# A transformer block on one core: the MLP's row preparation from batch 6 on, rearranged between ScalarE, VectorE and GpSimd

## The chip, the core and the metric

The kernel runs on one core of a Trainium2 chip. A core has five engines that run at the same time, each through its own list of instructions in order: TensorE (PE in the profile; PEld is its loading of weights), VectorE (DVE), ScalarE (ACT), GpSimd (POOL) and SyncE (SP), which here issues the DMA transfers. They wait for each other through semaphores. SBUF is the on-chip memory of 128 partitions, PSUM the small memory into which TensorE writes its products.

The metric is the device time of one execution in microseconds, the median of several runs. Beside it stands one execution taken by the hardware profiler, from which every row below comes.

## The reference, cut to what matters

`x` is 16 batches of 256 tokens by 256 channels, `cond_1024` one vector of 256 per batch, `ctx_1024` 16 x 256 x 256. All is float32. The block is

```python
shift_a, scale_a, gate_a, shift_m, scale_m, gate_m = split(silu(c) @ W_mod + b_mod, 6)
x = x + gate_a * (self_attention(modulate(ln(x), shift_a, scale_a)) @ W_proj + b_proj)
x = x + cross_attention(ln(x), ln(context)) @ W_cproj + b_cproj
x_norm2 = ln(x) * (1 + scale_m) + shift_m          # one scale and one shift per batch and channel
h = gelu(x_norm2 @ W_mlp1 + b_mlp1)                # 256 -> 1024 channels
x = x + gate_m * (h @ W_mlp2 + b_mlp2)             # 1024 -> 256 channels
```

Both attentions have 16 heads. The change touches only the last three lines, for the batches 6 to 15.

## The kernel before, in words

**Precision.** TensorE multiplies in a reduced float32 format (fp32r). To come close to float32, each operand is split into a high part (the value cast to fp32r) and a low part (value minus high part, again cast), and a product is made of three: high x high, high x low, low x high. So every tile that goes into a product needs a cast and a subtraction first.

**Stages.** First the 32 attention units (self and cross for 16 batches) run in an order written out by hand; each cross unit writes its batch's rows to a DRAM buffer `x2d`. Then comes a bridge (the word list `BE`), in which the last attention unit and the MLP of the batches 0 to 2 are interleaved. Then a loop over chunks does the MLP from batch 3 on. A batch has four chunks of 256 hidden channels (`NCH` = 4); iteration (b,c) is chunk c of batch b. Each engine gets its instructions in exactly the order in which the program issues them, so the loop's order is the order on every queue.

**A chunk.** Iteration (b,c) issues, for the chunk list counted by i:

- `mlp_gelu(i+1)`: ScalarE reads the first product `ph` from PSUM twice, each time as two halves of 128x256, into `hf` (float32) and `hh` (fp32r, the high part); GpSimd makes `hl = hf - hh`, 128x512;
- `mlp_first(i+2)`: TensorE, 12 matmuls into `ph`, from the rows' parts (`wcross`, see below) and the first weights (`wself`). There are two PSUM buffers for `ph`, so the first product of chunk i+2 needs `mlp_gelu(i)` to be finished;
- `mlp_second(i-1)`: TensorE, 12 matmuls into `st` or `sp` (`s` in the rows; the batches alternate), from `hh`, `hl` and the second weights (`big`). After a batch's last chunk VectorE multiplies by the gate (`mt`, two instructions), adds (`y`), and SP stores the result.

**The rows of a batch.** What `mlp_first` needs is the batch's normalised, scaled and shifted rows, turned so that channels lie on partitions, as high and low part. They stand in two alternating places, `ROWS[b % 2]`, both parts of the tile `wcross`. They come about as follows:

1. `mlp_load` (SP): the batch's rows from `x2d` into `xt`, `x` in the rows;
2. `mlp_bias`: adds `cb`, a bias row that is the same for all tokens, to `xt` in place (one 128x512 instruction, GpSimd);
3. `mlp_stats`: VectorE's mean and variance (`st_m`, `mv_m`);
4. `ln.pow`: GpSimd makes 1/sqrt(variance + eps) (`rs_m`, two small instructions); `mlp_nb`: VectorE makes the negated mean times that (`nb_m`);
5. `ln.steps[2]("act")`: ScalarE normalises, two Identity activations 128x256 into `xn_m`;
6. the turn. For the batches up to 5 (`TURN` is 6) `mlp_T` turns by TensorE, scales by VectorE and casts the high part by ScalarE. From batch 6 on `mlp_turn` has VectorE transpose 32x32 blocks (two instructions, into `z`), and SP moves the blocks between partitions with four DMAs of 64 KB (`yT<-z`);
7. `mlp_turned`, from batch 6 on: VectorE scales and shifts `yT` back into `z` (two instructions 128x256), casts the high part (128x512) and subtracts for the low part (128x512).

Besides, `mlp_gates` (SP) loads the batch's gate rows `gm`, and `mlp_residual` has VectorE prepare `xmg = x + ` a gate row (128x512).

**The order around the change.** For d = 6 and later the steps before stood so: bias at (d-3,0) (for d = 6 at (3,1)), statistics one iteration later, power at (d-3,3), negated mean and normalise at (d-2,0), turn at (d-2,1), at the end of that iteration and behind the store, the gates and the next load on SP, `mlp_turned` at (d-1,0). The first product that reads the rows is issued at (d-1,2). In the profile every instruction has line 51, that of a helper that issues all of them; rows are told apart by tile names.

The functions that the diff touches, and what calls them:

Of the kernel before, what the change touches and what calls it, by code (L numbers as in the profile page):

```python
# [21 lines left out]
def pixart_block(  # L22
# [8 lines left out]
    B, N, H = x.shape  # L31
# [4 lines left out]
    KC = H // P  # L36
# [15 lines left out]
                return tc.keep_in_program_order(i) if self.on else i  # L52
            return issue

    E_ = {'CUT': 8, 'LN': {'s': 'pool', 'c': 'pool', 'q': 'pool'}, 'ON': (1, 1, 1), 'L0': -16, 'L1': 1, 'S0': -7, 'A0': 0, 'T0': 1, 'S1': 5, 'A1': 7, 'L2': 9, 'T1': 9, 'S2': 32, 'AP': 99, 'DV': (0, 1), 'HP': (1, 0), 'BZ': {}, 'AV': {1: [(1, 2), (1, 3)], 9: [(0, 0), (0, 1)]}, 'AHEAD': (0, 0, 0, 0, 0, 2), 'TW': {(21, 6): 'cb', (23, 5): 'u0', (23, 7): 'u1', (25, 2): 'u2', (27, 3): 'u3', (27, 7): 'h2a', (28, 0): 'l2 h0p u5', (28, 2): 'h1p', (28, 4): 'h3p', (28, 7): 'u4 u6', (29, 0): 'l3d', (29, 1): 'l0', (29, 2): 'l1', (29, 7): 'h5p', (30, 1): 'u7 h6d h7p', (30, 3): 'h4p', (31, 1): 'l4 l6d', (31, 2): 'l5d x2', (31, 4): 'l7', (31, 7): 'b2'}, 'BE': 'G0 av P g0 A1 G1 G2 N1 F7 g1 S0 PF s2 p2 G3 a2 aT aL G4 x3 b3 S1 S2 T2 C r0 G5 S3 G6 S4 s3 CF x4 F8 g2 G7 S5 F9 p3 S6 G8 a3 r1 G9 F10 G10 T3 g3 b4 S7 s4 F11 S8 S9 F12 G11 p4 a4 F13 r2 S10 G12 x5 x6', 'XP': 1, 'IL': 1, 'MF': 0, 'SH': 4, 'RAMP': 1, 'HA': 1, 'MP': 16, 'W': (7, 1, 0, 0), 'PRE': 'load L0a z0kp z0qp L0b silu b15 hik turn L0d brow bp lok T0t lg scale b6 lc sc1 ld2 L1a T0h one0 z1kp bro2 T0l hiv hiq shift b3 K0a L1b bk K0m bq loq K0h b1 L1d K0l Q0a L2a T1t T1h lp K0yp K0x Q0m T1l bv K1a lov Q0h K0w V0a Q0l K1b Q1a L2b Q0x Q1b Q0w Q1l K1y V0b Q0yp b7 K1l ld3', 'SL': {(-1, 0): 'wm one1 L2c z1qp', (-1, 1): 'T2t T2h V1a', (-1, 2): 'K1wp T2p', (-1, 3): 'ga K1xp L3a Q1yp V1b z2kp', (-1, 4): 'M0 Q1xp Q1wp pb L3b vone gs', (-1, 5): 'z2qp ld4', (-1, 6): 'K2a K2m L3p', (-1, 7): 'L3c cb lx gm', (0, 0): 'sp3 mods', (0, 1): 'sp0', (0, 3): 'sp1', (0, 4): 'sc2', (0, 6): 'one2', (1, 1): 'sp2', (1, 2): 'sp4'}}

    PE = InOrder(nc.tensor, True)
    ACT, DVE, POOL, SP = (InOrder(e, True) for e in (nc.scalar, nc.vector, nc.gpsimd, nc.sync))
# [51 lines left out]
    brow = const.tile([32, P], F32, name="brow")  # L110
# [11 lines left out]
    def split(hi, lo, src, eng=POOL, hp=0):  # L122
        (DVE, POOL, ACT)[E_['HP'][hp]].tensor_copy(hi, src) if E_['HP'][hp] < 2 else ACT.copy(hi, src)
        eng.tensor_tensor(lo, src, hi, ALU.subtract)
# [173 lines left out]
    wm = []  # L298
# [9 lines left out]
    gm = []  # L308
# [19 lines left out]
    def layernorm(src, name):  # L328
# [282 lines left out]
    def bc_t(ap):  # L611
        return ap.unsqueeze(1).to_broadcast([P, NT, H])
# [226 lines left out]
    M = {}  # L839
# [6 lines left out]
        SP.dma_start(m.xt, tok(X2d, b))  # L846
        m.ln = layernorm(lambda: m.xt, f"m{b}")

    def mlp_bias(b):
        POOL.tensor_tensor(M[b].xt, M[b].xt, bc_t(cb), ALU.add)  # L850

    def mlp_stats(b, power=False):
        M[b].ln.steps[0]()
        M[b].ln.steps[1](power)

    def mlp_nb(b):
        ln = M[b].ln
# [14 lines left out]
    def mlp_residual(b):  # L872
        m = M[b]
        m.xg = work.tile([P, NT, H], F32, tag="x1", name=f"xmg_{b}", bufs=7)
        DVE.tensor_tensor(m.xg, m.xt, bc_t(m.g[:, 1]), ALU.add)

    def mlp_T(b):

        m = M[b]
        pst = ps_gen(f"psT_m{b}", SHORT)  # L880
        for f in range(KC):
            for t in range(NT):
                PE.transpose(pst[:, f * N + t * P:f * N + (t + 1) * P],
                             m.ln.xn[:, t, f * P:(f + 1) * P], ident)
        y = work.tile([P, KC, N], F32, tag="y", name=f"xTf_m{b}", bufs=2)
        hi, lo = ROWS[b % 2]
        for f in range(KC):
            DVE.tensor_scalar(y[:, f], pst[:, f * N:(f + 1) * N], sc1[:, 1, f, b:b + 1],
                              cpT[:, 6 + f, b:b + 1], ALU.mult, ALU.add)
        if b in E_['DV']:  # L890
            DVE.tensor_copy(hi, y)
        else:
            for f in range(KC):
                ACT.activation(hi[:, f], pst[:, f * N:(f + 1) * N], AF.Identity,
                               bias=cpT[:, 6 + f, b:b + 1], scale=sc1[:, 1, f, b:b + 1])
        DVE.tensor_tensor(lo, y, hi, ALU.subtract)
        m.xT = (hi, lo)

    TURN = 6

    def mlp_turn(b):


        m = M[b]
        m.z = work.tile([P, 4, KC, NT * 32], F32, tag="xn", name=f"z_{b}", bufs=3)
        m.y = work.tile([P, 4, KC, NT * 32], F32, tag="y", name=f"yT_{b}", bufs=2)
        for t in range(NT):
            DVE.transpose(m.z[:, :, :, 32 * t:32 * t + 32].rearrange("p j k c -> p k j c"),
                          m.ln.xn[:, t].rearrange("p (k c j) -> p k j c", k=KC, j=4))
        for a in range(4):  # L910
            SP.dma_start(m.y[:, a].rearrange("p k c -> p (k c)"),
                         m.z[32 * a:32 * a + 32].rearrange("r j k c -> r j (k c)"))

    def mlp_turned(b):

        m = M[b]
        hi, lo = m.xT = ROWS[b % 2]
        for f in range(KC):
            DVE.tensor_scalar(m.z[:, :, f], m.y[:, :, f], sc1[:, 1, f, b:b + 1],
                              cpT[:, 6 + f, b:b + 1], ALU.mult, ALU.add)  # L920
        y = m.z.rearrange("p a k c -> p k a c")
        hi, lo = [w.rearrange("p k (a c) -> p k a c", a=4) for w in (hi, lo)]
        DVE.tensor_copy(hi, y)
        DVE.tensor_tensor(lo, y, hi, ALU.subtract)

    NCH = NF // 2

# [112 lines left out]
    u0, u1 = units[:2]  # L1040
# [4 lines left out]
    u2 = units[2]  # L1045
# [40 lines left out]
    u3 = units[3]  # L1086
# [12 lines left out]
    for i in range(3):  # L1099
        for n, f in (("b", f_b), ("hi", f_hi), ("lo", f_lo)):  # L1100
            word[n + "qkv"[i]] = lambda f=f, i=i: f(i)
    for w in E_['PRE'].split():
        word[w]()
    for p, ws in E_['SL'].items():
        at[p] += [word[w] for w in ws.split()]
    ACT.on, POOL.on, SP.on = E_['ON']
    tail = []
    for i in range(3):
        b = i if i < 2 else 0
        u = ahead_of_mlp(nu + i, b)  # L1110
        u.T, u.ln = [], []
        if i < 2:
            u.ln = [layernorm(lambda b=b: M[b].xt, f"m{b}")]
            u.T = [transposed(lambda u=u: u.ln[0].xn, f"m{b}", [sc1[:, 1, f, b:b + 1] for f in range(KC)],
                              bias=[cpT[:, 6 + f, b:b + 1] for f in range(KC)])]
# [153 lines left out]
    last, o, q = units[-1], units[-1].post, units[-2].post  # L1269
# [11 lines left out]
        done[w]() if w in done else tail_word(w)  # L1281
    for i, (b, c) in list(enumerate(chunks))[12:]:
        ACT.on = i < E_['AP']
        by_dma = [d if d < B and d >= TURN else None for d in range(b + 1, b + 4)]
        by_pe = b + 2 if b + 2 < TURN else None
        new, late = by_dma[2], int(by_dma[2] == TURN)
        if c == 2 and by_pe:
            M[by_pe].ln.pow()
        if c == 3 and new:
            M[new].ln.pow()  # L1290
        if c == 0 and by_dma[1]:
            mlp_nb(by_dma[1])
        if i + 1 < len(chunks):
            mlp_gelu(*chunks[i + 1])
        if c == 0 and b + 1 < B:
            (mlp_turned if by_dma[0] else mlp_T)(b + 1)
        if c == 0 and by_dma[1]:
            M[by_dma[1]].ln.steps[2]("act")
        if i + 2 < len(chunks):
            mlp_first(*chunks[i + 2])  # L1300
        mlp_second(*chunks[i - 1])
        if c == 0 and by_pe:
            mlp_bias(by_pe)
        if c == late and new:
            mlp_bias(new)
        if c == 1:
            if b + 1 < B:
                mlp_gates(b + 1)
            if TURN < b + 4 < B:
                mlp_load(b + 4)  # L1310
            if by_pe:
                mlp_stats(by_pe)
        if c == 3:
            if by_pe:
                mlp_apply(by_pe, "act")
            mlp_residual(b)
        if c == late + 1 and new:
            mlp_stats(new)
        if c == 1 and by_dma[1]:
            mlp_turn(by_dma[1])  # L1320
    mlp_second(*chunks[-1])


# [46 lines left out]
```

## Time and profile before

| | |
|---|---|
| runs | 739.8, 739.31, 736.55 us; median 739.31 us |
| profiled execution, its own time | 740.44 us |
| its span (first to last instruction) | 738.5 us |
| granted TensorE clock, mean | 0.995 |
| busy, whole span | PE 99%, PEld 87%, DVE 79%, ACT 77%, POOL 74% |
| instructions | 24953, of them 10112 matmuls |
| the same between 648.4 and 660.4 us (12 us, about a batch) | PE 11.65, DVE 9.26, ACT 7.60, POOL 7.78 us |

Shares of busy time are means over stages that differ. The chain that ended last is 85% PE, 7% DVE, 2% POOL and 2% DMA over the whole span; from 610 us to the end its largest shares are the first product `ph` 18.8%, DVE's `wcross` 11.4%, the second product in `st` 11.1%, the DMA `yT<-z` 10.8%, the second product in `s` 9.9%, DVE's `z` 8.3% and SP's queue 6.3%.

### The profile page before, as it was taken

To read this page: it belongs to the slowest core of one execution; us is meant where nothing else is said; L and a number is where in the kernel's file an instruction comes from. 1 tells how busy PE (TensorE), PEld (TensorE's weight loads), DVE (VectorE), ACT (ScalarE), POOL (GpSimd) and SP (SyncE) were. 2 spreads that over 40 slices of the span, in tenths; PEclk is the share of its full clock that TensorE was granted. 3 is DMA by queue.
4 is the path that set the end of the run, shared out by engine and by line. 5 is a ranking of instruction groups with operands and counts; after the bars stand their busy time and mean duration, and the time that the engine had idled before them with its cause. 6 is when DMAs were issued, how large, how long until landed. Compare 5 with 4: busy or idle time off the path is not lost.

```text
span 738.5 us, 24953 instructions
## 1 busy us (share of the span) xinstructions
PE 728.6 (99%) x10112; PEld 640.9 (87%) x10112; DVE 583.0 (79%) x1207; ACT 566.0 (77%) x983; POOL 547.6 (74%) x574
## 2 busy tenths in 40 slices
PE   9999999999999999999999999999999999999997
PEld 9798888888888888888888888888879999999897
DVE  4878888889888888988989898888736677686852
ACT  4268898888888888888888888898886676666563
POOL 6877678869687786968768799799648676657553
PEclk9989999999999999999999999999999999999999
DMA  6643433332433343243334434334113231423321
GB/s 192 208 157 132 149 128 128 148 113 108 159 131 133 132 144 132 103 169 126 127 136 148 143 134 176 141 120 173 48 59 92 73 95 58 115 65 108 79 66 58
DMA packets 67110, 90.56 MB, mean 123 GB/s; under 512 B 6194, under 2 KB 38740, under 8 KB 66996
## 3 DMA queue, kind: packets, MB, share of 16 engines
q1 hardware_dynamic: 66164, 86.88, 34.8%
q8 instruction: 80, 1.31, 0.7%
q0 software_dynamic: 560, 1.84, 0.7%
q10 hardware_dynamic: 272, 0.26, 0.1%
q14 instruction: 34, 0.28, 0.1%
HBM read 26.97 MB, written 8.46 MB: 48 GB/s over the span
## 4 chain that ended last, share of the span: by engine, by line
PE 85%; DVE 7%; POOL 2%; DMA 2%; issue 1%; SPq 1%; ACT 1%; DVEq 0%; POOLq 0%; ACTq 0%
PE s L51 16%; PE o L51 16%; PE st L51 13%; PE ph L51 5%; PE ps_qc L51 4%; PE ps_q L51 4%; PE ps_P_s L51 4%; PE ps_kc L51 3%; PE ps_k L51 3%; PE ps_v_c L51 3%; PE ps_v_s L51 2%; PE ps_P_c L51 2%; DVE wcross L51 2%; DMA yT<-z 2%; DVE z L51 1%
## 5 line engine op out<-in xcount | busy, mean ns | idle before, releaser
L51 DVE TENSOR_REDUCE mx<-s 128x2 f32<-128x512 f32 x504 | 324.9, 684 | 64.8 <-PE s L51 58.3
L51 ACT ACTIVATE pt<-st 128x1024 f32<-128x1024 f32 x252 | 259.0, 1028 | 18.1 <-PE st L51 8.8
L51 PE MATMUL s<-big 63*128 63x256 f32 (+1 forms) x1024 | 185.8, 299 | 0.4 <-DVE mx L51 0.2
L51 PEld LDWEIGHTS s<-big 63*128 63x128 f32 (+1 forms) x1024 | 133.7, 186 | 19.1 <-DVE l_kc L51 6.6
L51 PE MATMUL st<-big 64*128 64x256 f32 (+1 forms) x1024 | 134.6, 299 | 0.0
L51 POOL TENSOR_TENSOR hl<-hf,hh 128x512 fp32r<-128x512 f32 x64 | 89.1, 1396 | 48.5 <-ACT hh L51 48.4
L51 PE MATMUL o<-pt,v 128*32 128x256 f32 x2048 | 123.8, 382 | 0.0
L51 PEld LDWEIGHTS st<-big 64*128 64x128 f32 (+1 forms) x1024 | 96.5, 187 | 15.0 <-issue 12.8
L51 PEld LDWEIGHTS o<-pt,v 128*32 128x32 f32 x2048 | 60.0, 109 | 41.5
L51 PE MATMUL ph<-wcross,wself 128*128 128x256 f32 x672 | 89.2, 280 | 3.4 <-DVE wcross L51 3.0
L51 PEld LDWEIGHTS ph<-wcross,wself 128*128 128x128 f32 x672 | 81.8, 188 | 6.2 <-DVE wcross L51 3.9
L51 ACT ACTIVATE hf<-ph,bT 128x256 f32<-128x256 f32 x114 | 47.9, 473 | 32.4 <-PE ph L51 32.4
L51 ACT ACTIVATE hh<-ph,bT 128x256 fp32r<-128x256 f32 x114 | 48.0, 474 | 22.1 <-PE s L51 9.8
L51 ACT COPY oT<-o 128x512 f32<-128x512 f32 x63 | 37.0, 587 | 32.8 <-PE o L51 32.8
L51 PE MATMUL ps_kc<-xTh_c,wcross 64*128 64x256 f32 x256 | 46.5, 291 | 0.0
L51 PE MATMUL st<-big,hh 128*128 128x256 f32 x256 | 45.6, 278 | 0.0
L51 PE MATMUL s<-big,hh 128*128 128x256 f32 x256 | 45.3, 277 | 0.0
L51 PE MATMUL ps_v_c<-wcross,xTh_c 64*128 64x256 f32 x256 | 44.2, 292 | 0.0
L51 PE MATMUL ps_k<-xTh_s,wself 64*128 64x256 f32 (+1 forms) x232 | 43.7, 293 | 0.0
L51 PE MATMUL ps_q<-xTh_s,wself 64*128 64x256 f32 (+1 forms) x240 | 41.9, 293 | 0.0
L51 PE MATMUL ps_qc<-xTh_q,wcross 64*128 64x256 f32 x256 | 41.3, 281 | 0.0
L51 POOL TENSOR_SCALAR xn_c<-c,mv_c,rs_c 128x256 f32<-128x256 f32 x32 | 39.1, 1230 | 1.7
(238 smaller groups left out, 2167.2 us busy)
## 6 DMA issues: line engine op xcount, KB each, us to landing
big<-h_kc SPq DMA_DIRECT2D x32, 256.0 KB
big<-h_qc SPq DMA_DIRECT2D x32, 256.0 KB
big<-h_k SPq DMA_DIRECT2D x30, 256.0 KB
big<-h_q SPq DMA_DIRECT2D x29, 256.0 KB
g<-gd SPq DMA_DIRECT2D x16, 256.0 KB
c<-in_ctx_dram SPq DMA_DIRECT2D x16, 256.0 KB
big<-l_kc SPq DMA_DIRECT2D x16, 256.0 KB
big<-l_qc SPq DMA_DIRECT2D x16, 256.0 KB
```

The lines of the kernel that those rows point to most:

```text
L51: i = f(*a, **k)
```

## The change

For the batches from 6 on:

- `mlp_turned` becomes two functions. `mlp_scaled` keeps the scaling into `z` on VectorE. `mlp_rows` makes the high part on ScalarE, as two Identity activations that read `yT` and apply scale and shift themselves; the low part stays VectorE's subtraction. The cast on VectorE is gone.
- The bias of these batches is added by VectorE (`mlp_bias(b, DVE)`) where GpSimd did it.
- The order: bias at (d-3,0), statistics (d-3,1), power (d-3,2), negated mean (d-3,3), normalise and turn at (d-2,0), with the four DMAs now ahead of the store, the gates and the load on SP, scaling and rows at (d-2,3). The rows of batch b+2 are begun and finished in batch b.
- In the bridge `BE` the loads of batch 5 and 6 (`x5 x6`) are issued earlier, after `b4` and before `S7`, in place of at the end.

The core of the diff (the one-line change of the word list left out):

```diff
-    def mlp_bias(b):
-        POOL.tensor_tensor(M[b].xt, M[b].xt, bc_t(cb), ALU.add)
+    def mlp_bias(b, eng=POOL):
+        eng.tensor_tensor(M[b].xt, M[b].xt, bc_t(cb), ALU.add)
...
-    def mlp_turned(b):
-
+    def mlp_scaled(b):
         m = M[b]
-        hi, lo = m.xT = ROWS[b % 2]
         for f in range(KC):
             DVE.tensor_scalar(m.z[:, :, f], m.y[:, :, f], sc1[:, 1, f, b:b + 1],
                               cpT[:, 6 + f, b:b + 1], ALU.mult, ALU.add)
-        y = m.z.rearrange("p a k c -> p k a c")
-        hi, lo = [w.rearrange("p k (a c) -> p k a c", a=4) for w in (hi, lo)]
-        DVE.tensor_copy(hi, y)
-        DVE.tensor_tensor(lo, y, hi, ALU.subtract)
+
+    def mlp_rows(b):
+
+        m = M[b]
+        m.xT = ROWS[b % 2]
+        hi, lo = [w.rearrange("p k (a c) -> p k a c", a=4) for w in m.xT]
+        for f in range(KC):
+            ACT.activation(hi[:, f], m.y[:, :, f], AF.Identity,
+                           bias=cpT[:, 6 + f, b:b + 1], scale=sc1[:, 1, f, b:b + 1])
+        DVE.tensor_tensor(lo, m.z.rearrange("p a k c -> p k a c"), hi, ALU.subtract)
...
-        by_dma = [d if d < B and d >= TURN else None for d in range(b + 1, b + 4)]
+        ahead = [d if TURN <= d < B else None for d in range(b + 2, b + 4)]
         by_pe = b + 2 if b + 2 < TURN else None
-        new, late = by_dma[2], int(by_dma[2] == TURN)
         if c == 2 and by_pe:
             M[by_pe].ln.pow()
-        if c == 3 and new:
-            M[new].ln.pow()
-        if c == 0 and by_dma[1]:
-            mlp_nb(by_dma[1])
         if i + 1 < len(chunks):
             mlp_gelu(*chunks[i + 1])
-        if c == 0 and b + 1 < B:
-            (mlp_turned if by_dma[0] else mlp_T)(b + 1)
-        if c == 0 and by_dma[1]:
-            M[by_dma[1]].ln.steps[2]("act")
+        if c == 0:
+            if b + 1 < TURN:
+                mlp_T(b + 1)
+            if ahead[1]:
+                mlp_bias(ahead[1], DVE)
+            if ahead[0]:
+                M[ahead[0]].ln.steps[2]("act")
+                mlp_turn(ahead[0])
+        if c == 2 and ahead[1]:
+            M[ahead[1]].ln.pow()
+        if c == 3 and ahead[0]:
+            mlp_scaled(ahead[0])
         if i + 2 < len(chunks):
             mlp_first(*chunks[i + 2])
         mlp_second(*chunks[i - 1])
         if c == 0 and by_pe:
             mlp_bias(by_pe)
-        if c == late and new:
-            mlp_bias(new)
         if c == 1:
             if b + 1 < B:
                 mlp_gates(b + 1)
...
             if by_pe:
                 mlp_stats(by_pe)
+            if ahead[1]:
+                mlp_stats(ahead[1])
         if c == 3:
             if by_pe:
                 mlp_apply(by_pe, "act")
+            if ahead[1]:
+                mlp_nb(ahead[1])
+            if ahead[0]:
+                mlp_rows(ahead[0])
             mlp_residual(b)
-        if c == late + 1 and new:
-            mlp_stats(new)
-        if c == 1 and by_dma[1]:
-            mlp_turn(by_dma[1])
     mlp_second(*chunks[-1])
```

More of the change, by code (lines that the diff above doesn't have):

```diff
@@ L53, in __getattr__ @@
             return issue
-    E_ = {'CUT': 8, 'LN': {'s': 'pool', 'c': 'pool', 'q': 'pool'}, 'ON': (1, 1, 1), 'L0': -16, 'L1': 1, 'S0': -7, 'A0': 0, 'T0': 1, 'S1': 5, 'A1': 7, 'L2': 9, 'T1': 9, 'S2': 32, 'AP': 99, 'DV': (0, 1), 'HP': (1, 0), 'BZ': {}, 'AV': {1: [(1, 2), (1, 3)], 9: [(0, 0), (0, 1)]}, 'AHEAD': (0, 0, 0, 0, 0, 2), 'TW': {(21, 6): 'cb', (23, 5): 'u0', (23, 7): 'u1', (25, 2): 'u2', (27, 3): 'u3', (27, 7): 'h2a', (28, 0): 'l2 h0p u5', (28, 2): 'h1p', (28, 4): 'h3p', (28, 7): 'u4 u6', (29, 0): 'l3d', (29, 1): 'l0', (29, 2): 'l1', (29, 7): 'h5p', (30, 1): 'u7 h6d h7p', (30, 3): 'h4p', (31, 1): 'l4 l6d', (31, 2): 'l5d x2', (31, 4): 'l7', (31, 7): 'b2'}, 'BE': 'G0 av P g0 A1 G1 G2 N1 F7 g1 S0 PF s2 p2 G3 a2 aT aL G4 x3 b3 S1 S2 T2 C r0 G5 S3 G6 S4 s3 CF x4 F8 g2 G7 S5 F9 p3 S6 G8 a3 r1 G9 F10 G10 T3 g3 b4 S7 s4 F11 S8 S9 F12 G11 p4 a4 F13 r2 S10 G12 x5 x6', 'XP': 1, 'IL': 1, 'MF': 0, 'SH': 4, 'RAMP': 1, 'HA': 1, 'MP': 16, 'W': (7, 1, 0, 0), 'PRE': 'load L0a z0kp z0qp L0b silu b15 hik turn L0d brow bp lok T0t lg scale b6 lc sc1 ld2 L1a T0h one0 z1kp bro2 T0l hiv hiq shift b3 K0a L1b bk K0m bq loq K0h b1 L1d K0l Q0a L2a T1t T1h lp K0yp K0x Q0m T1l bv K1a lov Q0h K0w V0a Q0l K1b Q1a L2b Q0x Q1b Q0w Q1l K1y V0b Q0yp b7 K1l ld3', 'SL': {(-1, 0): 'wm one1 L2c z1qp', (-1, 1): 'T2t T2h V1a', (-1, 2): 'K1wp T2p', (-1, 3): 'ga K1xp L3a Q1yp V1b z2kp', (-1, 4): 'M0 Q1xp Q1wp pb L3b vone gs', (-1, 5): 'z2qp ld4', (-1, 6): 'K2a K2m L3p', (-1, 7): 'L3c cb lx gm', (0, 0): 'sp3 mods', (0, 1): 'sp0', (0, 3): 'sp1', (0, 4): 'sc2', (0, 6): 'one2', (1, 1): 'sp2', (1, 2): 'sp4'}}
@@ new lines, in pixart_block @@
+    E_ = {'CUT': 8, 'LN': {'s': 'pool', 'c': 'pool', 'q': 'pool'}, 'ON': (1, 1, 1), 'L0': -16, 'L1': 1, 'S0': -7, 'A0': 0, 'T0': 1, 'S1': 5, 'A1': 7, 'L2': 9, 'T1': 9, 'S2': 32, 'AP': 99, 'DV': (0, 1), 'HP': (1, 0), 'BZ': {}, 'AV': {1: [(1, 2), (1, 3)], 9: [(0, 0), (0, 1)]}, 'AHEAD': (0, 0, 0, 0, 0, 2), 'TW': {(21, 6): 'cb', (23, 5): 'u0', (23, 7): 'u1', (25, 2): 'u2', (27, 3): 'u3', (27, 7): 'h2a', (28, 0): 'l2 h0p u5', (28, 2): 'h1p', (28, 4): 'h3p', (28, 7): 'u4 u6', (29, 0): 'l3d', (29, 1): 'l0', (29, 2): 'l1', (29, 7): 'h5p', (30, 1): 'u7 h6d h7p', (30, 3): 'h4p', (31, 1): 'l4 l6d', (31, 2): 'l5d x2', (31, 4): 'l7', (31, 7): 'b2'}, 'BE': 'G0 av P g0 A1 G1 G2 N1 F7 g1 S0 PF s2 p2 G3 a2 aT aL G4 x3 b3 S1 S2 T2 C r0 G5 S3 G6 S4 s3 CF x4 F8 g2 G7 S5 F9 p3 S6 G8 a3 r1 G9 F10 G10 T3 g3 b4 x5 x6 S7 s4 F11 S8 S9 F12 G11 p4 a4 F13 r2 S10 G12', 'XP': 1, 'IL': 1, 'MF': 0, 'SH': 4, 'RAMP': 1, 'HA': 1, 'MP': 16, 'W': (7, 1, 0, 0), 'PRE': 'load L0a z0kp z0qp L0b silu b15 hik turn L0d brow bp lok T0t lg scale b6 lc sc1 ld2 L1a T0h one0 z1kp bro2 T0l hiv hiq shift b3 K0a L1b bk K0m bq loq K0h b1 L1d K0l Q0a L2a T1t T1h lp K0yp K0x Q0m T1l bv K1a lov Q0h K0w V0a Q0l K1b Q1a L2b Q0x Q1b Q0w Q1l K1y V0b Q0yp b7 K1l ld3', 'SL': {(-1, 0): 'wm one1 L2c z1qp', (-1, 1): 'T2t T2h V1a', (-1, 2): 'K1wp T2p', (-1, 3): 'ga K1xp L3a Q1yp V1b z2kp', (-1, 4): 'M0 Q1xp Q1wp pb L3b vone gs', (-1, 5): 'z2qp ld4', (-1, 6): 'K2a K2m L3p', (-1, 7): 'L3c cb lx gm', (0, 0): 'sp3 mods', (0, 1): 'sp0', (0, 3): 'sp1', (0, 4): 'sc2', (0, 6): 'one2', (1, 1): 'sp2', (1, 2): 'sp4'}}
```

## The prediction

> **What bounds the kernel now.** The page gives PE 99% busy, but for a stage of its own (all instructions carry line 51, so I go by tiles) the timeline of PE decides. Columns: start, length, engine, operation, output<-inputs, count, and in brackets the idle time before. The program issues, for each chunk, the first product of the chunk two ahead (`ph`, 12 matmuls) and the second product of the chunk before (12 more): I call that a slot, and write (b,c) for the one in which iteration (b,c) runs. Its `ph` is that of chunk (b,c+2).
>
> ```profile
> 612.71 1.84 PE L51 MATMUL ph<-wcross,wself 128*128 128x256 f32 x12
> ...
> 618.47 1.52 PE L51 MATMUL ph<-wcross,wself 128*128 128x256 f32 x12
> 621.19 1.52 PE L51 MATMUL ph<-wcross,wself 128*128 128x256 f32 x12
> 624.14 0.35 PE L51 MATMUL ph<-wcross,wself 128*128 128x256 f32 x1
> 624.78 1.56 PE L51 MATMUL ph<-wcross,wself 128*128 128x256 f32 x11 [0.28 <-DVE wcross L51]
> 627.59 1.58 PE L51 MATMUL ph<-wcross,wself 128*128 128x256 f32 x12
> 630.42 1.58 PE L51 MATMUL ph<-wcross,wself 128*128 128x256 f32 x12
> ...
> 719.31 1.52 PE L51 MATMUL ph<-wcross,wself 128*128 128x256 f32 x12
> ```
>
> 612.71 is the first chunk of batch 6, 719.31 that of batch 15. An unhindered slot is 618.47 to 621.19 = 2.72, a batch 10.88. At 624.14 batch 7 begins: one matmul runs, then PE waits for `wcross`, the rows' high and low parts from VectorE. Nine batches take 719.31 - 612.71 = 106.60 instead of 9 x 10.88 = 97.92: **8.68 us are lost**. PE is also slower for a time after some stops (627.59 to 630.42 is 2.83); it runs so in three of the nine batches, batch 7 shown, 12 slots x 0.11 = 1.3 of the 8.7. The rest is 0.8 a batch.
>
> Next the waits between 600 and 720, and one turn of VectorE's timeline with SP's issues.
>
> ```profile
> DVE z L51 <- DMA yT<-z: 31.4, 10, 4.8
> ```
> ```profile
> 616.78 0.15 DVE L51 SCALAR_TENSOR_TENSOR nb_m<-mv_m,rs_m 128x2 f32<-128x2 f32 x1
> ...
> 670.71 1.33 DVE L51 CAST wcross<-z 128x512 fp32r<-128x512 f32 x1
> 672.07 0.69 DVE L51 TENSOR_TENSOR wcross<-z,wcross 128x512 fp32r<-128x512 f32 x1
> 672.68 0.75 DVE L51 TENSOR_TENSOR mt<-s,gm 128x256 f32<-128x256 f32 x2
> 673.46 1.44 DVE L51 TENSOR_TENSOR y<-xmg,mt 128x512 f32<-128x512 f32 x1
> 674.83 0.74 DVE L51 BATCH_NORM_STATS2 st_m<-x 128x6 f32<-128x256 f32 x2
> 675.49 0.30 DVE L51 BATCH_NORM_AGGREGATE mv_m<-st_m 128x2 f32<-128x6 f32 x2
> 675.70 1.13 DVE L51 STREAM_TRANSPOSE z<-xn_m 128x256 f32<-128x256 f32 x2
> 676.76 0.65 DVE L51 TENSOR_TENSOR xmg<-x,gm 128x512 f32<-128x512 f32 x1
> ...
> 682.29 1.82 DVE L51 TENSOR_SCALAR z<-yT,sc,cpT 128x256 f32<-128x256 f32 x2 [3.71 <-DMA yT<-z]
> ...
> 706.25 0.43 DVE L51 CAST wcross<-z 128x512 fp32r<-128x512 f32 x1
> ```
> ```profile
> 653.16 2.49 SPq L51 DMA_DIRECT2D yT<-z  x4
> ...
> 675.94 0.39 SPq L51 DMA_DIRECT2D x<-x2d  x1
> 676.86 2.49 SPq L51 DMA_DIRECT2D yT<-z  x4
> ```
> ```profile
> 657.45 1.40 DVE L51 TENSOR_SCALAR z<-yT,sc,cpT 128x256 f32<-128x256 f32 x2 [2.57 <-DMA yT<-z]
> ```
>
> VectorE stands 31.4 us in ten waits for the turned tile, in order: behind the waiting scaling are the cast, the low part, the residual (`mt`, `y`), the statistics and the next batch's transposes. That closes a ring without PE: transposes 1.13, four issues on SP 2.49, landing, scaling, cast, low part, `mt`, `y`, statistics, transposes. From 653.16 + 2.49 = 655.65 the data came 1.80 later; 676.86 + 2.49 to 682.29 is 2.94. One turn is on average 106.60 / 9 = 11.84, 0.96 over PE's 10.88. The ring, not PE, sets the batches 6 to 15.
>
> **The change part by part.** Batches 6 to 15, ten of each.
>
> *Rows a slot earlier and outside the ring.* The rows of b+2 are turned in (b,0) and finished in (b,3); their first `ph` is in (b+1,2), three slots = 8.16 later. Before, the finish was asked for at (b+1,0), two slots ahead, and was late even for that. The stop of PE at `wcross` should go: at most 8.68.
>
> *Transposes and four DMAs in (b,0).* They follow ScalarE's normalise, and on SP they now go ahead of the store, the gates and the x load, the last of which was issued at 675.94, just ahead of the four at 676.86. ScalarE around a normalise:
>
> ```profile
> 618.62 0.84 ACT L51 ACTIVATE hh<-ph,bT 128x256 fp32r<-128x256 f32 x2 [0.47 <-PE s L51]
> 619.35 1.09 ACT L51 ACTIVATE xn_m<-x,nb_m,rs_m 128x256 f32<-128x256 f32 x2
> 620.33 0.83 ACT L51 ACTIVATE hf<-ph,bT 128x256 f32<-128x256 f32 x2
> 621.34 0.84 ACT L51 ACTIVATE hh<-ph,bT 128x256 fp32r<-128x256 f32 x2 [0.17 <-PE s L51]
> ```
>
> Slot (6,0) begins at 618.47, the normalise ends at 620.44 = +1.97. Transposes +2.0 to +3.1, SP to +5.6, landing 1.8 to 2.9 later: +7.4 to +8.5, against (b,3) at +8.16. The data are there from 0.8 before to 0.3 after the slot that uses them.
>
> *High part from VectorE to ScalarE.* VectorE loses a cast of 0.43 to 1.33 (mean below). ScalarE gains two Identity activations 128x256 from SBUF; the trace has none of that output, the nearest is the normalise's pair, 1.09 (a pair of `hh` from PSUM, 0.84, is the lower bound; the upper is 2 x 597 ns = 1.19). They sit in a slot where ScalarE has 2.72 - 1.68 = 1.04 free; the row at 621.34 shows that the same insertion cost the next `hh` nothing (it still waited 0.17 for PE). Cost 0 on the path, cover: that idle time. Without it, 0.05 to 0.15 a batch, 0.5 to 1.5.
>
> What is queued behind: the high part waits for the landing, and behind it ScalarE has the GELUs. If the data come L after the start of (b,3), then L + 1.09 + 0.84 + 0.84 must be under two slots, 5.44, when PE needs the PSUM buffer that `hh` frees: **L under 2.67 costs nothing**. Behind VectorE's scaling stand the negated mean for the next normalise, low part, residual, bias, transposes.
>
> *Bias from GpSimd to VectorE, and the other groups* (window 600 to 720; columns: count, busy, mean ns, idle before):
>
> ```profile
> L51 DVE TENSOR_SCALAR z<-yT,sc,cpT 128x256 f32<-128x256 f32 x20 | 12.7, 678 | 31.4 <-DMA yT<-z 31.4
> L51 DVE TENSOR_TENSOR y<-xmg,mt 128x512 f32<-128x512 f32 x11 | 12.5, 1137 | 0.4
> L51 DVE SCALAR_TENSOR_TENSOR nb_m<-mv_m,rs_m 128x2 f32<-128x2 f32 x9 | 10.2, 1130 | 0.9 <-POOL rs_m L51 0.9
> L51 DVE CAST wcross<-z 128x512 fp32r<-128x512 f32 x10 | 9.7, 969 | 1.0
> L51 DVE TENSOR_TENSOR wcross<-z,wcross 128x512 fp32r<-128x512 f32 x10 | 8.9, 886 | 0.3
> L51 DVE TENSOR_TENSOR xmg<-x,gm 128x512 f32<-128x512 f32 x11 | 8.2, 747 | 0.0
> ```
> ```profile
> L51 ACT ACTIVATE xn_m<-x,nb_m,rs_m 128x256 f32<-128x256 f32 x19 | 10.4, 597 | 0.0
> ```
> ```profile
> L51 POOL TENSOR_TENSOR hl<-hf,hh 128x512 fp32r<-128x512 f32 x41 | 57.7, 1406 | 32.1 <-ACT hh L51 32.0
> L51 POOL TENSOR_TENSOR x<-x,cb 128x512 f32<-128x512 f32 x8 | 10.4, 1302 | 0.0
> ```
>
> The nearest row to the bias on VectorE is `xmg` (same shape, one broadcast input): 0.65 free, mean 0.75; as upper bound the mean of `y`, 1.14. VectorE's busy time barely moves: -0.97 + 0.75. GpSimd loses 1.30 a batch, off the path. The bias also brings a wait into VectorE's queue, ahead of the transposes: for the x load of b+3, asked for in (b-1,1) behind the four issues. Counted from (b-1,0) those end at +5.6; store, gates and load take some 1.4 to issue (the row at 675.94 has 0.39 for one), landing after 1.8 to 2.9 like the turned tile, so +8.8 to +9.9, and the bias stands at +10.88: 0, at worst 0.5 to 1 if the load is late.
>
> The new ring is transposes 1.13, SP 2.49, landing 1.8, scaling 2 x 0.68, negated mean 1.13, low part 0.89, `xmg` 0.75, bias 0.75 = **10.3** (10.7 with 1.14); residual (`mt`, `y`) and statistics, 3.2, now run while the DMAs do. 10.3 is under 10.88, barely. All the longer forms pay waits: the cast is 0.43 or 1.33, and here its end, 672.04, follows that of an `hl` on GpSimd, 671.76:
>
> ```profile
> 670.30 1.46 POOL L51 TENSOR_TENSOR hl<-hf,hh 128x512 fp32r<-128x512 f32 x1 [0.17 <-ACT hh L51]
> ```
> ```profile
> L51 DVE TENSOR_SCALAR z<-yT,sc,cpT x20: 401/413/1501, 608.1 to 716.6; 128x256 f32<-128x256 f32 x20
> ```
>
> The second row (least, median and greatest ns) gives 0.83 for a scaling that meets nobody. With it, 0.15 for the negated mean (616.78), 0.69 for the low part and 0.65 for `xmg` and the bias, the ring is 8.4.
>
> The Trainium skill (SBUF — State Buffer, section Who interferes with whom) says that a VectorE instruction with two SBUF inputs, or in a two-port mode, and a GpSimd instruction that reads SBUF lock each other out. By that rule the bias is no freer on VectorE, and each of the ring's two-input instructions could wait out an `hl`; the trace agrees for the cast above.
>
> *Statistics (b,1), power (b,2), negated mean (b,3).* The power stands in front of an `hl` on GpSimd; GpSimd idles 32.1 us before its 41 `hl`, 0.8 each, and a product needs `hl` more than a slot later: 0, at most the 0.8 once that cover is gone, and then still not PE's.
>
> *x loads of 5 and 6 issued earlier, batches 3 and 4.* Two loads go ahead of a store on SP that nobody waits for; VectorE's bias of 6 and 7 comes behind the rows of batch 4 and 5: 0, bounds -0.5 to +1 for the first turn.
>
> **Sum.** 740.44 (the profiled execution; span 738.5 and 1.94 around it) - 8.68 + 0.4 for late landings (my estimate: one like that of 682.29, 1.1 over the usual, of which a third is not absorbed) = 732.2. The median of the runs, 739.31, lies 1.1 below the profiled one; I take 0.7 of that: **731.5**.
>
> **Rivals.**
> 1. *Slow pace of PE.* In the first fence the pace goes to 2.83 at a stop and stays. The last interruption that the change leaves is PE's transposes for batch 5:
>
> ```profile
> 595.92 0.60 PE L51 MATMUL psT_m<-ident,xn_m 128*128 128x128 f32 x4
> ```
> Without stops the pace found there would hold to the end, 46 slots: 46 x 0.11 = 5, so 731.5 + 5 = **736.5**. For: 3 of 9 batches are slow now. Against: the pace behind this interruption was the fast one (618.47 to 621.19).
>
> 2. *The wait moves to ScalarE.* Landing over +2.67 in some batches stops the GELUs, then PE. The ring at 11.2 instead of 10.3 would lose 0.3 x 9 less the 2.7 of slack at first, hence little; at 11.5, 5.6 - 2.7 = 3: **734.5**. For: ring at 10.3 to 10.7 and the first turn is late; against: 1.8 as the usual landing.
>
> 3. *Slower: the ring of lock waits.* Scaling, low part and bias each wait out an `hl` of 1.3, and landings are 1 late: 8.4 + 3.9 + 1 = 13.3; (13.3 - 10.88) x 9 - 2.7 = 19, so **750.5**. It decides from a turn of 12.6 (8.68 + 3.7 + 2.7 = 15.1 over nine). For: the cast at 670.71 and the greatest scaling, 1501 ns. Against: GpSimd is free half the time, and `xmg` took 0.65 in the turn shown. This is the case in which the Trainium skill's rule (SBUF — State Buffer, Who interferes with whom) strikes at every meeting.
>
> 4. *Nothing gained*: the ring stays near 11.84 + 0.3: **740**. For: the same landing stays in the ring. Against: the cast, `mt`, `y` and statistics are out of it.
>
> **How the numbers follow.** Forecast 0.62 (own range 728.5 to 734); slow pace 0.13; ScalarE's wait 0.12; lock waits 0.08; nothing 0.05. From 728.5 to 737 lie 0.59 of the first, 0.09 of the second and 0.11 of the third: 0.8. What a measurement can tell from no change is 0.5%, 735.6 to 743.0. Faster: 0.60 of the forecast, 0.05 of rival 1, 0.10 of rival 2 = 0.75. Slower: rival 3 and 0.02 of rival 4 = 0.10. Same: the rest, 0.15.
>
> **What would show it.** First `ph` of the batches 10.88 apart, no wait of PE for `wcross`; scaling at most 1.3 after (b,3) begins; ScalarE's new `wcross` about 0.55 each; `x` on VectorE 0.65 to 1.1. It is wrong if ScalarE waits for `yT` by more than 2.7 after its slot, or if batches repeat at over 11.3.

## The result, and the profile after

The changed kernel takes 730.36 us (median; 728.96 to 731.23), the one before, measured beside it, 737.93: the ratio is 0.9894, 95% interval 0.9861 to 0.9927. The profiled execution took 728.96 with a span of 727.2, against 740.44 and 738.5.

TensorE's timeline of the changed kernel, same columns as before: the first chunks of the batches 6, 7, 8 and 15, and the slots in between.

```profile
610.03 1.52 PE L51 MATMUL ph<-wcross,wself 128*128 128x256 f32 x12
612.75 1.52 PE L51 MATMUL ph<-wcross,wself 128*128 128x256 f32 x12
...
620.91 1.52 PE L51 MATMUL ph<-wcross,wself 128*128 128x256 f32 x12
...
631.79 1.52 PE L51 MATMUL ph<-wcross,wself 128*128 128x256 f32 x12
...
707.95 1.52 PE L51 MATMUL ph<-wcross,wself 128*128 128x256 f32 x12
```

No row has a bracket: TensorE waits for nothing, and each of the nine batches from 610.03 to 707.95 takes 10.88, together 97.92. Before it was 106.60, so the 8.68 are gone to the last hundredth. The two profiles differ by 11.48 in all; the rest was there before the changed stage begins, as the chain of waits shows, before and after, for the same attention unit:

```profile
545.10 1.91 PE o L51 x32
```
```profile
542.46 1.91 PE o L51 x32
```

2.64 of the difference stands here already, in code that nobody changed; such differences between single executions are why the gain is read from the stage (8.68) and from the medians (7.6 to the 737.93 beside it, 9.0 to the 739.31 of before). The profiled execution before is slower than all four runs of its kernel, the one after is the fastest of its four, so the 11.48 overstates the gain.

The waits between 600 and 720 after:

```profile
DVE z L51 <- DMA yT<-z: 21.3, 10, 3.9
...
DVE wcross L51 <- ACT wcross L51: 6.0, 6, 1.1
...
DVE x L51 <- DMA x<-x2d: 2.0, 5, 0.7
...
ACT wcross L51 <- DMA yT<-z: 0.7, 1, 0.7
```

VectorE still waits 21.3 us for the turned tile, but TensorE for nobody. Groups after, VectorE and then ScalarE:

```profile
L51 DVE TENSOR_SCALAR z<-yT,sc,cpT 128x256 f32<-128x256 f32 x20 | 11.5, 617 | 21.3 <-DMA yT<-z 21.3
L51 DVE TENSOR_TENSOR xmg<-x,gm 128x512 f32<-128x512 f32 x12 | 10.4, 863 | 0.0
...
L51 DVE TENSOR_TENSOR x<-x,cb 128x512 f32<-128x512 f32 x8 | 8.7, 1090 | 2.0 <-DMA x<-x2d 2.0
L51 DVE TENSOR_TENSOR wcross<-z,wcross 128x512 fp32r<-128x512 f32 x10 | 8.2, 825 | 6.1 <-ACT wcross L51 6.0
L51 DVE SCALAR_TENSOR_TENSOR nb_m<-mv_m,rs_m 128x2 f32<-128x2 f32 x9 | 3.6, 403 | 3.0 <-POOL rs_m L51 2.9
```
```profile
L51 ACT ACTIVATE wcross<-yT,cpT,sc 128x256 fp32r<-128x256 f32 x20 | 10.9, 597 | 0.8 <-DMA yT<-z 0.7
```

The new activation takes 597 ns, exactly the normalise's. The bias on VectorE takes 1.09 in the mean, GpSimd's took 1.30.

### The profile page after: what moved, and what is told of

The parts are those of the page before. It is cut to its first block, busy times and chain, and to the rows that moved or that the text cites. A ratio compares the mean times of both kernels' runs of the same rounds, so it can differ in the third digit from the quotient of the medians.

```text
span 727.2 us, 24962 instructions
## 1 busy us (share of the span) xinstructions
PE 720.1 (99%) x10112; PEld 634.7 (87%) x10112; DVE 572.0 (79%) x1207; ACT 573.8 (79%) x1003; POOL 532.1 (73%) x564
## 4 chain that ended last, share of the span: by engine, by line
PE 94%; POOL 3%; DVE 2%; issue 1%; ACT 1%; POOLq 0%; ACTq 0%
PE s L51 18%; PE o L51 16%; PE st L51 16%; PE ph L51 10%; PE ps_q L51 4%; PE ps_qc L51 4%; PE ps_P_s L51 4%; PE ps_kc L51 3%; PE ps_v_c L51 3%; PE ps_k L51 3%; PE ps_v_s L51 2%; PE ps_P_c L51 2%; PE ps_h L51 1%; PE psT_q L51 1%; PE psA_s L51 1%; POOL hl L51 1%
## 5 line engine op out<-in xcount | busy, mean ns | idle before, releaser
L51 POOL TENSOR_TENSOR hl<-hf,hh 128x512 fp32r<-128x512 f32 x64 | 87.5, 1369 | 63.0 <-ACT hh L51 60.9
L51 PE MATMUL ph<-wcross,wself 128*128 128x256 f32 x672 | 85.5, 277 | 0.0
L51 PE MATMUL ps_q<-xTh_s,wself 64*128 64x256 f32 (+1 forms) x240 | 39.8, 282 | 0.0
```

The costliest lines, as they stand in the source:

```text
L51: i = f(*a, **k)
```

## The experiments

All ran beside the kernel before. "Batches 6 to 15" is the time from the first chunk of batch 6 to that of batch 15 in the profiled execution, 106.60 before and 97.92 after; "ratio" is to the kernel before, with its 95% interval.

| run | batches 6 to 15 | median | ratio |
|---|---|---|---|
| order alone | 97.92 | 731.09 | 0.9871 (0.9821 to 0.9922) |
| new order, cast on VectorE | 97.92 | 730.92 | 0.9883 (0.9833 to 0.9932) |
| new order, bias on GpSimd | 97.92 | 729.91 | 0.9872 (0.9846 to 0.9899) |
| new, x loads of 5 and 6 late | 97.92 | 730.49 | 0.9876 (0.9860 to 0.9891) |
| old order, high part on ScalarE | 103.65 | 736.71 | 0.9944 (0.9913 to 0.9975) |
| old order, bias on VectorE | 105.37 | 736.76 | 0.9969 (0.9936 to 1.0001) |
| old order, no bias | 99.87 | 734.46 | 0.9928 (0.9897 to 0.9959) |
| old, four more issues | 115.11 | 749.39 | 1.0123 (1.0096 to 1.0150) |
| new, four more issues | 107.84 | 741.66 | 1.0028 (1.0014 to 1.0042) |
| the same, x load first | 101.82 | 732.52 | 0.9898 (0.9856 to 0.9940) |
| new, turn late | 104.59 | 738.08 | 0.9975 (0.9962 to 0.9989) |
| new, one more matmul a batch | 100.14 | 733.85 | 0.9919 (0.9902 to 0.9936) |

**Which part of the change.** Both moves of work undone in the new order (or the cast alone, or the bias alone):

```diff
-            ACT.activation(hi[:, f], m.y[:, :, f], AF.Identity, ...)     # twice
+        DVE.tensor_copy(hi, m.z.rearrange("p a k c -> p k a c"))
...
-                mlp_bias(ahead[1], DVE)
+                mlp_bias(ahead[1])
```

> The changed kernel with both moves of work undone: the high part is a cast on VectorE and the bias is on GpSimd, in the new order. Theory (ring): the new ring holds transposes, SP, landing, scaling, cast, low part, residual's preparation, together about 10.2 us without the bias, under 10.88: the whole gain remains, 730 to 731. Rival (the gain is that VectorE is relieved of the cast): about 738.

> The changed kernel with only the high part undone: the cast is on VectorE, the bias on VectorE too. Theory (ring): the ring gets longer by the cast, 0.4 to 1.0, to 10.4 to 11.0 against the 10.88 of TensorE, with 2.7 us of slack over ten batches: 730 to 732. Rival (the cast on VectorE was the cause): 737 or more.

> The changed kernel with only the bias undone: GpSimd adds it, at the same place in the program. Theory (ring): the ring is shorter by the bias, 0.65 to 1.05, but TensorE already sets the pace: no change against the changed kernel, 730 to 731. Rival (GpSimd's bias holds up VectorE or the low parts of the hidden values): 732 to 735.

All three have 97.92 in the stage, to the hundredth, and medians within 1.2 us of each other. The new order alone gives the whole gain; in that order, where the cast and the bias are done adds nothing to it. None is faster than the changed kernel by more than the runs scatter. Nor do the earlier loads matter:

```diff
-  ... g3 b4 x5 x6 S7 ... S10 G12
+  ... g3 b4 S7 ... S10 G12 x5 x6
```

> The changed kernel with the loads of batch 5 and 6 back at the end of the bridge. Theory: a load of 256 KB issued there lands about 4 us later, which is when VectorE's bias of batch 6 wants it; a wait of up to 1 us delays nothing that TensorE needs: 729 to 731, no change. Rival (VectorE's queue is held up at its bias, then the rows of batch 5): 731 to 733.

730.49, no change; VectorE's bias of batch 6 did not wait. (It stands at 587.16 in that run, without a bracket.)

**The two moves of work in the old order.**

```diff
 # high part on ScalarE, in mlp_turned
-        DVE.tensor_copy(hi, y)
+        for f in range(KC):
+            ACT.activation(hi[:, f], m.y[:, :, f], AF.Identity, bias=..., scale=...)
 # in another kernel: the bias
-            mlp_bias(new)
+            mlp_bias(new, DVE)
```

> The kernel before with one part alone: the high part of the rows made by ScalarE (two Identity activations), everything else in the old order. Theory (the ring transposes - SP - landing - scaling - cast - low part - residual - statistics - transposes sets the batches 6 to 15): the cast, 0.97 us in the mean, leaves the ring, a turn goes from 11.84 to about 10.9, and 6 to 8 of the 8.7 us come back: 730 to 732 on the scale of 738. ScalarE now waits for the turned tile in front of its GELUs, which could give back 1 to 3: 735 at most. Rival (the new order alone is what helps; the rows are asked for too late in the program): 737 to 739.

> The kernel before with the other part alone: the bias of batch 6 and later added by VectorE at its old place in the program. Theory (ring): the bias lies in the ring, between the residual and the statistics, and each turn grows by 0.7 to 1.1 us: 745 to 749 on the scale of 738. Rival (VectorE stands 31 us idle in this stage, so 10 us more on it are hidden): 738, no change.

Both missed. With the high part on ScalarE the stage took 103.65, where 6 to 8 us back would have been 98.6 to 100.6. TensorE's timeline and ScalarE's row at its second stop:

```profile
632.12 1.52 PE L51 MATMUL ph<-wcross,wself 128*128 128x256 f32 x12
636.02 1.68 PE L51 MATMUL ph<-wcross,wself 128*128 128x256 f32 x12 [1.01 <-ACT hh L51]
638.95 1.58 PE L51 MATMUL ph<-wcross,wself 128*128 128x256 f32 x12
641.77 1.58 PE L51 MATMUL ph<-wcross,wself 128*128 128x256 f32 x12
```
```profile
632.44 1.10 ACT L51 ACTIVATE wcross<-yT,cpT,sc 128x256 fp32r<-128x256 f32 x2 [2.05 <-DMA yT<-z]
```

ScalarE, waiting for the turned tile, kept the GELUs from TensorE: the wait moved from the product's rows to its PSUM buffer. And after the stop TensorE ran at 2.83 a slot to the end; 27 slots x 0.11 = 3 of the 5.7 lost are that. The other 2.7 are the stops, inside the 1 to 3 us that the expectation had allowed for ScalarE's wait; the slow pace it had not.

The bias on VectorE, which should have made each turn of the ring 0.7 to 1.1 longer, did not lengthen the stage (105.37). The rival had named that number, no change, but for the reason that VectorE's idle time hides the bias. To see why, the bias was left out:

```diff
-            mlp_bias(new)
+            pass
```

> The kernel before without the bias of batch 6 and later (it is left out altogether, so these batches lack the cross projection's bias row). Question: why the bias on VectorE did not lengthen the old ring. Theory: GpSimd's bias stood directly ahead of an hl, and VectorE's scaling and cast waited both out; without it the cast falls from 0.97 to about 0.6 and the scaling by 0.1, so a turn of the ring loses about 0.9, six to seven turns of it are paid: 732 to 735 on the scale of 739. Rival (GpSimd's bias was off the path, as the prediction had it, and the old turn is set by something else): 738 to 740.

It came out as expected, 734.46 and 99.87. Without GpSimd's bias 6.73 us come back, 0.75 a turn; VectorE's bias in its stead costs 105.37 - 99.87 = 5.5, 0.6 a turn, so it was not hidden: two costs of about the same size were exchanged. VectorE's groups without the bias and with VectorE's bias (before: scaling 678, cast 969):

```profile
L51 DVE TENSOR_SCALAR z<-yT,sc,cpT 128x256 f32<-128x256 f32 x20 | 8.7, 478 | 26.3 <-DMA yT<-z 26.3
L51 DVE CAST wcross<-z 128x512 fp32r<-128x512 f32 x10 | 7.4, 742 | 1.4 <-PE s L51 0.5
```
```profile
L51 DVE TENSOR_SCALAR z<-yT,sc,cpT 128x256 f32<-128x256 f32 x20 | 11.8, 632 | 29.5 <-DMA yT<-z 29.5
...
L51 DVE CAST wcross<-z 128x512 fp32r<-128x512 f32 x10 | 6.2, 619 | 1.0
```

In the kernel before, GpSimd's bias runs beside the scaling, and the `hl` that follows it (670.30, shown in the prediction) beside the cast of 670.71:

```profile
668.84 1.29 POOL L51 TENSOR_TENSOR x<-x,cb 128x512 f32<-128x512 f32 x1
```
```profile
669.58 1.02 DVE L51 TENSOR_SCALAR z<-yT,sc,cpT 128x256 f32<-128x256 f32 x2 [2.55 <-DMA yT<-z]
```

Without the bias, two scalings of 0.20 and a cast of 0.23 less are 0.63 of the 0.75. So GpSimd's bias was in the ring, though nobody waited for its result: it made VectorE's instructions longer. The lengths are measured; that the engines wait for a memory port that they share (a port wait, below) is inferred from which rows overlap. It agrees with the Trainium skill (SBUF — State Buffer, Who interferes with whom), which counts scalings and casts in a two-port mode among the instructions that GpSimd blocks.

**How long the rings are.** Four more DMAs on SP ahead of the turn's four, in both kernels:

```diff
+        for a in range(4):
+            SP.dma_start(scr[b, a]..., m.z[32 * a:32 * a + 32]...)
         for a in range(4):
             SP.dma_start(m.y[:, a]..., m.z[32 * a:32 * a + 32]...)
```

> The kernel before with the same four more DMAs on SP ahead of the four of the turned tile. Theory (the ring sets the batches): every turn grows by the whole 2.4 us, 9 x 2.4 = 22, so 757 to 763 on the scale of 738. Rival (the waits of VectorE for the turned tile are mostly idle time that nobody pays): under 745.

> The changed kernel with four more DMAs of the same size on SP ahead of the four that bring the turned tile (they copy the same data to an unused buffer in DRAM). Each issue takes 0.6 us, so the data land 2.4 us later. Theory (the ring still exists and is only a little under TensorE's 10.88): a turn goes to about 12.4 to 12.8; after 2.7 us of slack the rest is paid: (12.6 - 10.88) x 9 - 2.7 = 13, so 741 to 746. Rival (the rows have three slots, 8.16 us, of slack and 2.4 of it can be spent every batch): 730 to 731.

These four took 1.7 and not 2.4 to issue. The old kernel's turn went from 11.84 to 115.11 / 9 = 12.79, by 0.95, and the run stayed under the expected 757 to 763: the ring is real, but nearly half of the 1.7 was taken up. VectorE's groups show where:

```profile
L51 DVE TENSOR_SCALAR z<-yT,sc,cpT 128x256 f32<-128x256 f32 x20 | 12.3, 651 | 48.1 <-DMA yT<-z 48.1
L51 DVE CAST wcross<-z 128x512 fp32r<-128x512 f32 x10 | 6.1, 608 | 1.0
```

The cast is 0.61 in place of 0.97. So the port waits depend on when VectorE arrives, and an added delay is partly paid out of them.

The changed kernel lost 9.92 us with the four more issues, close to the 13 expected, but by another road. Waits in that run, between 600 and 720:

```profile
ACT wcross L51 <- DMA yT<-z: 24.4, 10, 3.9
DVE x L51 <- DMA x<-x2d: 11.8, 8, 1.8
...
PE ph L51 <- ACT hh L51: 5.5, 5, 1.9
```

VectorE's bias waited for the x load, which SP issues last, and the transposes stand behind the bias. The next run put that load ahead of the turn on SP:

```diff
+                if TURN < b + 4 < B and b > 3:
+                    mlp_load(b + 4)
                 mlp_turn(ahead[0])
...
-            if TURN < b + 4 < B:
+            if b == 3:
                 mlp_load(b + 4)
```

> The changed kernel with the four more issues on SP, and with the x load of batch b+4 issued ahead of the turn's DMAs in place of behind them. Question: which ring set the pace of the run with four more issues. Theory: not the turned tile's ring (8.4 + 1.8 = 10.2, under 10.88) but that of the x load, which SP issued last and for which VectorE's bias waited 1.1 to 1.7 us a turn (1.15 + 1.7 + 2.5 + 1.6 + 4.0 + 0.7 = 11.7): with the load first the batches go back to 10.88 but for one or two late landings, 730 to 733. Rival (the turned tile's ring): 740 to 742, no better.

732.52, so it was the x load's ring that had been pushed over TensorE's 10.88, not the turned tile's. (TensorE itself needed 11.31 a batch for most of this run, see the pace below, so the run does not hold the turned tile's ring against 10.88 at every turn; its shortest turn there, from one high part on ScalarE at 626.35 to the next at 636.59, is 10.24.) From the end of its issue to its use the load needs 3.8 in the changed kernel without more issues, SP's row and VectorE's:

```profile
623.76 0.40 SPq L51 DMA_DIRECT2D x<-x2d  x1
```
```profile
627.99 1.26 DVE L51 TENSOR_TENSOR x<-x,cb 128x512 f32<-128x512 f32 x1 [0.73 <-DMA x<-x2d]
```

**Where the turn stands.** In the changed kernel, the turn back at the end of the second iteration:

```diff
                 M[ahead[0]].ln.steps[2]("act")
-                mlp_turn(ahead[0])
...
             if ahead[1]:
                 mlp_stats(ahead[1])
+            if ahead[0]:
+                mlp_turn(ahead[0])
```

> The changed kernel with the turn alone put back to the end of the second iteration of a batch, behind the residual, the statistics and, on SP, the store, the gates and the load; the rows are still finished in the fourth. Theory (ring): residual and statistics, 2.7 to 3.2 us, come back into the ring, a turn of about 12.5 to 13, and (12.7 - 10.88) x 9 - 2.7 = 14: 741 to 748, slower than the kernel before. Rival (the rows only have to be finished earlier in the program than before): 730 to 733.

738.08, so most of the gain is gone, though the loss is smaller than expected (741 to 748): the gain needs the turn's place ahead of the residual and the statistics. The run moves the turn back in SP's list too, but SP is not what delays it: in the turn below it ends the x load's issue at 649.01, before the transposes end at 649.53. The ring was not the expected 12.5 to 13 either. VectorE between two scalings of a stretch without stops, and at the last stop:

```profile
642.88 0.73 DVE L51 TENSOR_SCALAR z<-yT,sc,cpT 128x256 f32<-128x256 f32 x2 [4.34 <-DMA yT<-z]
...
645.81 0.82 DVE L51 TENSOR_TENSOR mt<-s,gm 128x256 f32<-128x256 f32 x2
646.66 0.93 DVE L51 TENSOR_TENSOR y<-xmg,mt 128x512 f32<-128x512 f32 x1
647.52 0.74 DVE L51 BATCH_NORM_STATS2 st_m<-x 128x6 f32<-128x256 f32 x2
648.18 0.29 DVE L51 BATCH_NORM_AGGREGATE mv_m<-st_m 128x2 f32<-128x6 f32 x2
...
653.85 0.74 DVE L51 TENSOR_SCALAR z<-yT,sc,cpT 128x256 f32<-128x256 f32 x2 [4.32 <-DMA yT<-z]
...
667.58 0.74 DVE L51 TENSOR_SCALAR z<-yT,sc,cpT 128x256 f32<-128x256 f32 x2 [6.66 <-DMA yT<-z]
```
```profile
660.95 2.49 SPq L51 DMA_DIRECT2D yT<-z  x4
```

The turn is 653.85 - 642.88 = 10.97, only 0.09 over TensorE's 10.88. What the late turn takes away is time in hand: in the batches without a stop ScalarE's high part starts 2.1 to 2.8 after its slot, in the changed kernel mostly 0.9. So a late landing stops TensorE here. At 667.58 the tile is used 4.14 after the end of SP's issue (660.95 + 2.49), at 653.85 it was 1.80; at the other stop it was 3.41. In the changed kernel 3.04 once (608.93 + 2.49 to 614.46) cost nothing. VectorE's groups in the late run:

```profile
L51 DVE TENSOR_SCALAR z<-yT,sc,cpT 128x256 f32<-128x256 f32 x20 | 7.4, 411 | 49.4 <-DMA yT<-z 49.4
L51 DVE TENSOR_TENSOR wcross<-z,wcross 128x512 fp32r<-128x512 f32 x10 | 6.9, 692 | 2.9 <-ACT wcross L51 2.9
L51 DVE TENSOR_TENSOR x<-x,cb 128x512 f32<-128x512 f32 x9 | 6.2, 685 | 0.0
L51 DVE SCALAR_TENSOR_TENSOR nb_m<-mv_m,rs_m 128x2 f32<-128x2 f32 x9 | 1.4, 154 | 0.0
```

Every one of them is close to its shortest length; the port waits have gone. Of the 6.67 us that this run loses in the stage two stops are 2.6; the pace of 2.83 a slot, which holds through all of it, is 36 x 0.11 = 4.0.

**How late the tile may be.** The runs with four more issues give the delay of TensorE against L, here the time from the start of slot (b,3) to ScalarE's high part. The example is batch 11 of the run with the load behind:

```profile
662.97 1.52 PE L51 MATMUL ph<-wcross,wself 128*128 128x256 f32 x12
665.69 1.52 PE L51 MATMUL ph<-wcross,wself 128*128 128x256 f32 x12
670.50 1.80 PE L51 MATMUL ph<-wcross,wself 128*128 128x256 f32 x8 [1.92 <-ACT hh L51]
```
```profile
667.90 1.09 ACT L51 ACTIVATE wcross<-yT,cpT,sc 128x256 fp32r<-128x256 f32 x2 [3.94 <-DMA yT<-z]
```

L is 667.90 - 662.97 = 4.93, and the second slot after begins 4.81 and not 2.72 after the first: a delay of 2.09. So for the batches at this pace (3.12 is from the run with the load first):

| L | 1.74 | 2.64 | 3.12 | 3.59 | 3.80 | 4.06 | 4.21 | 4.93 |
|---|---|---|---|---|---|---|---|---|
| delay | 0 | 0 | 0.27 | 0.74 | 0.95 | 1.21 | 1.36 | 2.09 |

The delay is L - 2.85 once that is positive. In the changed kernel L is 0.87 in eight of nine batches (ScalarE is then still at the GELU before, the tile is there) and 1.67 in one: it has 1.2 to 2 us in hand.

**The pace of TensorE.**

```diff
+        if c == 0 and b >= TURN:
+            busy(1, ps_gen(f"ps_re{b}", SHORT))
```

> The changed kernel with one more 128x128 matmul of TensorE at the start of each batch from batch 6 on (its result is not used). It costs 0.1 to 0.3 each, 1 to 3 us. Question: what switches TensorE between 2.72 and 2.83 us a slot. Theory: any instruction of another length, or a stop, draws the pace anew, so of ten batches some three are slow, the others not. Rival (only a stop of TensorE does it): all ten batches at the same pace, 733 at most if it is the fast one.

The theory fails: every batch takes 11.13, that is 10.88 and 0.25 for the added matmul (two rows of 128x128 in the trace), and none has the slow pace (the median, 733.85, is 0.9 above what the rival allowed). But the rival, that only a stop changes the pace, does not hold without exception, and the exception is in this same run, ahead of its first added matmul:

```profile
593.02 1.58 PE L51 MATMUL ph<-wcross,wself 128*128 128x256 f32 x12
...
595.85 0.60 PE L51 MATMUL psT_m<-ident,xn_m 128*128 128x128 f32 x4
...
599.02 1.52 PE L51 MATMUL ph<-wcross,wself 128*128 128x256 f32 x12
```

The pace is 2.83 up to the four transposes of batch 5, which have no bracket, and 2.72 behind them. Counted by the distance from one matmul to the next, over all the profiled executions from 575 us on, the pace changes 22 times, 21 of them at a stop. That a stop can bring the slow pace stands in the run with the load first, whose one stop is at 618.65, of 0.27: afterwards all slots are 2.83 to the end.

```profile
652.68 1.58 PE L51 MATMUL ph<-wcross,wself 128*128 128x256 f32 x12
655.51 1.58 PE L51 MATMUL ph<-wcross,wself 128*128 128x256 f32 x12
```

Its loss of 3.90 us in the stage is 0.3 for the stop and 33 x 0.11 = 3.6 for the pace behind it. Neither pace shows in the granted clock. A stretch at 2.72 (the kernel before) and one at 2.83 (the run with the turn late); the third number from the end is the clock:

```profile
585.00:624.00 39.00, 38.97 (x342) 38.65 (x340) 27.37 (x50) 27.66 (x66) 29.91 (x27) 1.00 0.29 76
```
```profile
640.00:655.00 15.00, 15.00 (x130) 15.00 (x129) 7.20 (x19) 10.29 (x25) 8.58 (x9) 1.00 0.38 109
```

## Why the prediction was right, and where not

**The diagnosis held.** The ring over VectorE, SP and the landing set the batches: a delay on SP in it lengthens the turns (by 0.95 of the 1.7 put in), and the order that takes residual and statistics out of it brings TensorE to its own 10.88. The amount lost, 8.68, was read from the distances of the first chunks and came back whole. The bracket of idle time at `wcross`, 3.0 us in all, would have shown a third of it.

**The sum.** The allowance of 0.4 for late landings was not needed: one landing in nine was late (L 1.67) and under the limit. The forecast lies 1.1 above the median. That the slow pace stayed away was a chance that the sum did not contain and rival 1 priced: no run shows what decides it.

**"L under 2.67 costs nothing"** was mis-sized by 0.2: the runs give 2.85. The mechanism is the one that was argued.

**"GpSimd loses 1.30 a batch, off the path"** was wrong. In the old order GpSimd's bias cost 0.75 a turn through the waits of scaling and cast. The step looked at who waits for the bias's result, and not at what runs beside it, though the prediction had read the cast's row beside an `hl` in just this way. It did not show in the total, because the new order leaves the ring too short to matter.

**The new ring as a sum of means, 10.3**, was the wrong kind of sum. The means contain port waits that belong to the old moments of arrival. The late turn ran 10.97 with residual and statistics in the ring; without the 2.8 that its rows give for these (0.82 + 0.93 + 0.74 + 0.29), that is 8.2, next to the other sum, 8.4 from the shortest rows. How much of the port waits comes on top depends on the moment: the bias ran 0.68 to 1.83 in the changed kernel.

**The bias's wait for the x load** was put at 0 with a landing after 1.8 to 2.9. It took 3.8, and the bias waited five times, 0.7 at most. Of the two rings this one is the nearer to becoming the bound: with four more issues it was the one that did.

**High part on ScalarE: 0 on the path.** Right in the new order, 0.60 each. (The trace before did have a nearer row than the normalise's: ScalarE makes the high part of the batches up to 5, from PSUM, in 1.02 a pair, for instance at 598.08. It lies inside the stated bounds.) But the move brings nothing either, and in the old order ScalarE's wait for the tile stopped TensorE, as the second rival had it for the new one.

**The rivals.** ScalarE's wait and the slow pace did not come in the changed kernel; both came in runs whose tile was later. The ring of lock waits did not come: VectorE's bias took up to 1.83, 1.15 over its shortest, and TensorE waited for nothing all the same.

What stays open: why TensorE goes on at 2.83 after some stops and at 2.72 after others, and why it once changed without one. The granted clock is 1.00 at both paces. Not run either is the other half of the new order by itself: the turn early, with the rows finished at their old place.

## What to carry to other kernels

A busy share of 99% can hide a bound elsewhere: compare the distance of like events from one repetition to the next with the distance inside an undisturbed one. When a ring of engines and DMAs is longer than the busiest engine's work, look for what stands in it only by its place in a queue (here residual and statistics ahead of the transposes) and put the long transfer first; moving single instructions to another engine was worth less here. Count a ring from the shortest rows of its instructions and keep the waits for shared ports apart, since they shrink or grow with the moment of arrival.

## What the runs showed of the hardware that was not expected

TensorE has two paces for the same matmuls, 2.72 and 2.83 us for 24, at the same granted clock in the rows. In these runs it changed at stops of TensorE (21 of 22 changes; the other came at four transposes, without a stop), not at an added matmul of another length (none of ten batches), and it lasted: a stop of 0.27 us was followed by 33 slow slots in the stage, 3.6 us. A stop can therefore cost over ten times its own length. The changed kernel, whose TensorE did not stop in the stage, kept 2.72 through all 36 slots.
